# Layer-1 batch statistics of a four-layer graph network: one aggregation for each group of four batches in place of two for each batch

## The chip, the cores and the metric

The kernel runs on one core of a Trainium2 chip. Its time is the device time of one execution, in microseconds (us); the kernel before takes 2887.32 us, the median of three runs from 2887.09 to 2894.89. One further execution was profiled; its span is 2889.8 us. In the text the engines carry the names of the profile: PE (matrix multiply; PEld is its weight load), DVE (vector), ACT (scalar), POOL (GpSimd), SP (the queue that issues most transfers).

## What is computed

Four layers, each `x = x + layer(relu(layernorm(x)))`, on x of shape (128 batches, 128 nodes, 128 features), with a 0/1 adjacency of the same leading shape. The change lies in layer 1, whose reference, cut to what matters, is

```python
D = jnp.abs(x[:, :, None, :] - x[:, None, :, :])
h = jnp.einsum('bijc,oc->bijo', D, W1) + b1      # 64 outputs for each pair of nodes
m = jnp.mean(h, axis=(0, 1, 2))                  # over all batches and all pairs
v = jnp.mean((h - m) ** 2, axis=(0, 1, 2))
h = (h - m) / jnp.sqrt(v + EPS) * g1 + be1
...                                              # leaky relu, score, softmax, aggregation
```

The mean and the variance of h run over all 128 batches and all 128 x 128 pairs (i, j), so no h can be normalised before the last one exists. That is why the kernel has a first stage that only makes h and its statistics.

## The kernel before, in words

**Stages.** The first stage (about 80 to 1600 us of the span) computes h for every pair, keeps its statistics and writes h to DRAM (`HP`), and beside that runs layer 0 for the batches ahead. A short stretch of small operations (L804 to L841) folds the statistics into one scale and one bias. The second stage (about 1610 to 2400 us) reads h back and does the rest of layer 1; layers 2 and 3 follow.

**Tiles of the first stage.** D is symmetric, so for each batch only the distances k = 1 to 64 between i and j (mod 128) are made: the upper half of the partitions holds k = 1 to 32, the lower half 33 to 64. A batch has NT = 4 tiles of KC = 8 distances; i counts the tiles of all batches (512), b = i // 4 is the batch and t = i % 4 the tile in it. Four batches (G = 4) make a group of 16 tiles, the unit in which layer 0 runs. Since k = 64 meets each pair twice, it counts with half the weight of the others; it sits in the last 128 columns of the last tile of a batch.

For each tile, with the step names of the code:

- `d` (L585) takes the difference of x and its shifted copy. In tiles 1 and 3 of a batch POOL does it, in tiles 0 and 2 DVE; tile 0 uses a maximum in place of the difference. DVE reads x out of PSUM (`XP`, two tiles, one for each pair of batches, in turns), POOL out of SBUF.
- `abs` (L624, ACT) takes the absolute value in place; tile 0 of a batch has none.
- `hp` (L595 and, in tile 0 alone, also L598; PE) multiplies by W1 into one of two PSUM buffers (`big`, bufs=2), so hp of tile i can start when `hs` of tile i-2 has emptied its buffer.
- `hs` (L608, ACT) copies the result to SBUF.
- `st` (L615 to L620, DVE) takes its statistics: two bn_stats for each tile, of 512 columns each. In the last tile of a batch the second one covers only 384 columns, a third one takes the last 128 (k = 64), and two bn_aggr turn the nine triples of the batch into a mean and a variance of all and of the last k alone (`ST1[:, b, 0]`, `ST1[:, b, 1]`).
- `out` (SP) writes the batch's h to DRAM.

Other steps of the stage: for each pair of batches, number n, `xp<n>` (L652, PE, transposes x into XP), `xe<n>` (L656, ACT, copies it to SBUF), `again<n>` (L669, POOL, appends the first 64 columns again), `pw<n>` (L660, PE, a product with W1 into another part of the same XP tile), `xw<n>` (L664, ACT, reads that part). For each group, layer 0: `mask`, `rs`, `most`, `share`, `rso`, `m8`, `rsx` on POOL, `mv`, `deg`, `o`, `mvo`, `on`, `end`, `mvx`, `per` on DVE, `hn`, `hT`, `maskT`, `hw`, `oc`, `h1` on ACT, `pt`, `pm`, `ph`, `po` on PE.

**What sets the order.** Every step is entered in a list with an engine, an assumed cost in us, the steps it must follow, a rank (when it is due) and its work. `_ordered` (L113) runs a list schedule over that: it always takes the step that could start first by the assumed costs, the lower rank at a tie, and emits them in that order. Nothing is sorted again afterwards: each engine works off its queue in that order and waits at the head of it. The costs are entries in the planner only; they change no instruction, but they decide the order of every queue.

In the steady part the order repeats from group to group. With tiles 0 to 15 for a group, negative numbers for tiles of the group before, xw<1> for the second pair of batches of this group, <2> and <3> for those of the next, and (1), (2), (3) for layer 0 of one, two and three groups ahead, the order of the kernel before is

```
DVE  d0 st-4 d2 st-3 o(1) st-2 mvo(1) st-1 d4 st0 st1 mv(2) d6 st2 deg(2) on(1) st3 d8 end(1) st4 mvx(1)
     st5 d10 per(2) st6 st7 d12 st8 st9 d14 st10 st11
ACT  hs0 abs3 hs1 oc(1) hs2 xw<1> hs3 abs5 abs6 hs4 abs7 hs5 hs6 hn(2) hs7 abs9 hs8 hs9 abs10 abs11 h1(1)
     hT(2) hs10 h1(1) xe<2> abs13 hs11 hs12 abs14 maskT(2) xw<2> abs15 hw(2) hs13 hs14 xe<3> abs17 hs15 abs18
PE   hp0 hp1 hp2 pw<1> hp3 hp4 hp5 hp6 hp7 hp8 hp9 pt(2) hp10 hp11 xp<2> hp12 pm(2) ph(2) pw<2> hp13 hp14
     xp<3> po(2) hp15
POOL d1 again<1> d3 rso(1) d5 d7 rs(2) d9 most(2) d11 rsx(1) d13 share(2) d15 again<2> mask(3) m8(3)
```

In both kernels xw<2> (ACT) is emitted just after the d0 of the next group (DVE) and waits for it, and that d0 waits for pw<2> (PE): all three touch the same PSUM tile XP.

Of the kernel before, what the change touches and what calls it, by code (L numbers as in the profile page):

```python
# [9 lines left out]
F32 = mybir.dt.float32  # L10
# [7 lines left out]
P = 128  # L18
G = 4
# [8 lines left out]
KH = 32  # L28
# [6 lines left out]
NT = KH // KC  # L35
# [131 lines left out]
def tile_gnn_stack(ctx: ExitStack, tc: tile.TileContext, a: dict, out: bass.AP):  # L167
    nc = tc.nc
    NB = a["x"].shape[0]
    NG = NB // G  # L170

    const = ctx.enter_context(tc.tile_pool(name="const", bufs=1))
    res = ctx.enter_context(tc.tile_pool(name="res", bufs=1))
    small = ctx.enter_context(tc.tile_pool(name="small", bufs=4))
# [7 lines left out]
    def sm(name, tag="sm"):  # L182
        return psum.tile([P, G, P], F32, tag=tag, bufs=banks[tag], name=name)
# [28 lines left out]
    M8 = [res.tile([P, G, P], U8, tag=f"m{g}", name=f"m{g}") for g in range(NG)]  # L212
    MV1 = res.tile([P, NG, G, 2], F32, name="MV1")
    RS1 = res.tile([P, NG, G], F32, name="RS1")
    ST1 = res.tile([P, NB, 2, 2], F32, name="ST1")
    ST2 = res.tile([P, NG, 6], F32, name="ST2")

    def rsqrt(dst, var):

        nc.gpsimd.tensor_scalar(dst, var, EPS, None, op0=OP.add)  # L220
        nc.gpsimd.tensor_tensor(dst, dst, mhalf[:, 0:1].to_broadcast(list(dst.shape)), OP.pow)  # L221
# [35 lines left out]
    with tc.tile_pool(name="c0", bufs=1) as c0, tc.tile_pool(name="p0", bufs=2) as p0:  # L257
# [311 lines left out]
        def step(name, engine, cost, after, rank, work, takes=(), gives=()):  # L569
            steps.append((name, engine, cost, after, takes, gives, rank, work))  # L570

        XE, XW, diffs, linear, halves, stats = {}, {}, {}, {}, {}, {}

        def difference(i):

            b, t = divmod(i, NT)
            xe, k = XE[b // 2], b % 2
            on_pool = t in ON_POOL
            d = p0.tile([P, 2, KC, P], F32, tag=f"d{int(on_pool)}", name="d")
            x = xe[:, k, 0:P] if on_pool else XP[b // 2 % 2][:, k, :]  # L580
            ahead = xe[:, k, 1 + KC * t:]
            ahead = bass.AP(tensor=ahead.tensor, offset=ahead.offset,
                            ap=[list(ahead.ap[0]), [KH, 2], [1, KC], [1, P]])
            eng = nc.gpsimd if on_pool else nc.vector
            eng.tensor_tensor(d, ahead, x[:, None, None, :].to_broadcast([P, 2, KC, P]),  # L585
                              OP.max if t == BY_MAX else OP.subtract)
            diffs[i] = d.rearrange("p h k i -> p h (k i)")

        def products(i):
            d = diffs.pop(i)  # L590
            hp = linear[i] = big("hp").rearrange("p a b -> p (a b)")
            by_max = i % NT == BY_MAX
            for c in range(0, KC * P, 512):
                for hh in range(2):
                    nc.tensor.matmul(hp[64 * hh:64 * hh + 64, c:c + 512], w1T2 if by_max else w1T,  # L595
                                     d[:, hh, c:c + 512], start=True, stop=not by_max, skip_group_check=True)
                for hh in range(2 * by_max):
                    nc.tensor.matmul(hp[64 * hh:64 * hh + 64, c:c + 512], XW[i // NT // 2][:, i // NT % 2, :],  # L598
                                     both_t.rearrange("p h k i -> p h (k i)")[:, hh, c:c + 512],
                                     start=False, stop=True, skip_group_check=True)  # L600

        def evacuate(i):

            b, t = divmod(i, NT)
            if t == 0:
                halves[b] = p0.tile([P, NT, KC * P], F32, name="hs", bufs=3)
                stats[b] = small.tile([P, 9, 6], F32, name="st")
            nc.scalar.copy(halves[b][:, t, :], linear.pop(i))  # L608

        def statistics(i):  # L610

            b, t = divmod(i, NT)
            last = t == NT - 1
            hs, st = halves[b][:, t, :], stats[b]
            nc.vector.bn_stats(st[:, 2 * t, :], hs[:, 0:512])  # L615
            nc.vector.bn_stats(st[:, 2 * t + 1, :], hs[:, 512:1024 - P * last])  # L616
            if last:
                nc.vector.bn_stats(st[:, 8, :], hs[:, 1024 - P:])
                nc.vector.bn_aggr(ST1[:, b, 0, :], st.rearrange("p a b -> p (a b)"))
                nc.vector.bn_aggr(ST1[:, b, 1, :], st[:, 8, :])  # L620
                del stats[b]

        def absolute(i):
            nc.scalar.activation(diffs[i], diffs[i], AF.Abs)  # L624

        def pairs(i):

            b, t = divmod(i, NT)
            n, by_max = b // 2, t == BY_MAX
            engine, cost, rank = ("Pool", 4.25, i - 3) if t in ON_POOL else ("DVE", 2.2, i - 2)  # L630
            step(("d", i), engine, cost, [("again", n), ("d", i - 2), ("hp", i - 4)], rank, lambda: difference(i))
            if not by_max:
                step(("abs", i), "ACT", 1.8, [("d", i)], i - 1, lambda: absolute(i))
            step(("hp", i), "PE", 3.44 if by_max else 1.72,
                 [("d" if by_max else "abs", i), ("hp", i - 1), ("hs", i - 2)] + [("xw", n)] * by_max,
                 i, lambda: products(i))
            step(("hs", i), "ACT", 0.9, [("hp", i), ("hs", i - 1)]
                 + [("st", i - 2 * NT - 1), ("out", b - 3)] * (t == 0), i + 1, lambda: evacuate(i))
            step(("st", i), "DVE", 1.8 if t == NT - 1 else 1.2, [("hs", i), ("st", i - 1)], i + 2,
                 lambda: statistics(i))  # L640
            if t == NT - 1:
                step(("out", b), "SP", 0.4, [("hs", i)], i + 1.5, lambda: nc.sync.dma_start(HP[b], halves[b]))
# [154 lines left out]
        for i in range(NT * NB):  # L797
            pairs(i)
# [5 lines left out]
    with tc.tile_pool(name="bn", bufs=1) as bn:  # L804


        w_all, w_last, n = 2.0 * KH * P, -1.0 * P, 1.0 * NB * P * P
        last = bn.tile([P, 1], F32, name="last")
        nc.vector.memset(last[0:64, :], 0.0)
        nc.vector.memset(last[64:128, :], w_last)  # L810

        def fold_sum(t):

            acc = bn.tile([P, NB], F32, name="acc")
            nc.vector.tensor_scalar(acc, t[:, :, 0], w_all, None, op0=OP.mult)
            nc.vector.scalar_tensor_tensor(acc, t[:, :, 1], last[:, 0:1], acc, op0=OP.mult, op1=OP.add)
            tot = bn.tile([P, 1], F32, name="tot")
            nc.vector.tensor_reduce(tot, acc, AX.X, OP.add)
            pf = sm("pf")
            nc.tensor.matmul(pf[:, 0, 0:1], fold.rearrange("p a b -> p (a b)"), tot, start=True, stop=True)  # L820
            got = bn.tile([P, 1], F32, name="got", bufs=2)
            nc.vector.tensor_scalar(got, pf[:, 0, 0:1], 1.0 / n, None, op0=OP.mult)
            return got

        m = fold_sum(ST1[:, :, :, 0])
        dev = bn.tile([P, NB, 2], F32, name="dev")
        nc.vector.tensor_scalar(dev, ST1[:, :, :, 0], m[:, 0:1], None, op0=OP.subtract)
        nc.vector.tensor_tensor(dev, dev, dev, OP.mult)
        nc.vector.tensor_tensor(dev, dev, ST1[:, :, :, 1], OP.add)
        v = fold_sum(dev)  # L830
        mm = bn.tile([P, 1], F32, name="mm")
        nc.vector.tensor_tensor(mm, m, m, OP.mult)
        nc.vector.scalar_tensor_tensor(v, mm, NB * P / n, v, op0=OP.mult, op1=OP.add)
        scale1 = const.tile([P, 1], F32, name="scale1")
        bias1 = const.tile([P, 1], F32, name="bias1")
        rsqrt(scale1, v)
        nc.vector.tensor_tensor(scale1, scale1, g1, OP.mult)

        nc.vector.tensor_tensor(m, m, b1, OP.add)
        nc.vector.tensor_tensor(bias1, b1, m, OP.subtract)  # L840
        nc.vector.scalar_tensor_tensor(bias1, bias1, scale1[:, 0:1], be1, op0=OP.mult, op1=OP.add)  # L841
# [8 lines left out]
    with tc.tile_pool(name="c1", bufs=1) as c1, tc.tile_pool(name="p1", bufs=2) as p1:  # L850
# [34 lines left out]
        for n in range(2):  # L885
            t = c1.tile([P, G, 1 + 2 * KH], F32, name=f"sk{n}")
# [683 lines left out]
```

## Time and profile before

| what | value |
|---|---|
| median of three runs | 2887.32 us |
| span of the profiled execution | 2889.8 us |
| busy share of the span: PE, DVE, ACT, POOL | 85%, 87%, 83%, 60% |
| first stage: DVE, ACT, POOL, PE busy in 1000 to 1500 us | 473.62, 459.35, 453.83, 450.03 us |
| bn_stats L615 x512, L616 x512, L618 x128 | 681, 642 and 276 ns each |
| bn_aggr L619 x128 (54 numbers for each partition) | 399 ns each |
| bn_aggr L620 x128 (6 numbers) | 124 ns each |
| second stage, 1700 to 2300 us | DMA busy all the time, 409 GB/s |

A group of instructions is named by its line, its engine and the tiles it writes and reads; st<-hs is the statistics' bn_stats, ST<-st the bn_aggr. Idle time of an engine is put down to the instruction that ended the wait. The chain of waits goes back from the last instruction, at each step to what released it, and is then told in order of time.

### The profile page before, as it was taken

Reading aid. Unit: us, or ns where it says so; the run is one execution under the profiler, and the core shown is the slowest. Engines: PE = TensorE matmul, PEld = TensorE weight load, DVE = VectorE, ACT = ScalarE, POOL = GpSimd, SP = SyncE. Lnnn points to the kernel's source line nnn. Section 1 sums busy time; section 2 is a strip of 40 time slices with the busy share of each in tenths; the row PEclk is TensorE's granted clock in tenths of the full one; section 3 lists DMA queues with packets and bytes.
Section 4 is the critical chain, followed back from the end, with each engine's and each line's share of the span. In section 5 each row is a group of like instructions: output and inputs, shape, how many; then the busy total and the mean of one; then the engine's idle time right before and its main releaser. Section 6 shows DMA issues by size and latency. Waiting matters only on the chain.

```text
span 2889.8 us, 41921 instructions
## 1 busy us (share of the span) xinstructions
PE 2469.7 (85%) x14517; PEld 1185.7 (41%) x14517; DVE 2520.0 (87%) x4949; ACT 2392.2 (83%) x2811; POOL 1729.1 (60%) x1613
## 2 busy tenths in 40 slices
PE   1899899999898989898989688888888886998897
PEld 1333333333333333333333234444444444777675
DVE  5799999999999999999999578888888885987886
ACT  1799998989899999999999678777877774988886
POOL 2899989898989899898988001101111104665552
PEclk8899999999999999999999899999999997999998
DMA  5555545454544444454544999999999971111210
GB/s 200 201 202 221 204 190 204 190 204 190 204 193 200 195 199 200 193 207 186 215 171 204 368 408 408 410 409 409 410 410 410 408 283 54 45 59 63 63 34 27
DMA packets 180083, 653.83 MB, mean 226 GB/s; under 512 B 30992, under 2 KB 99472, under 8 KB 129680
## 3 DMA queue, kind: packets, MB, share of 16 engines
q1 hardware_dynamic: 179280, 646.80, 56.3%
q10 hardware_dynamic: 576, 4.19, 0.4%
q8 instruction: 119, 1.95, 0.3%
q14 instruction: 108, 0.88, 0.1%
HBM read 338.14 MB, written 312.80 MB: 225 GB/s over the span
## 4 chain that ended last, share of the span: by engine, by line
PE 36%; ACT 23%; DMA 20%; DVE 12%; issue 5%; POOL 3%; SPq 0%; DVEq 0%; ACTq 0%; POOLq 0%
PE hp L595 17%; ACT d L624 11%; DMA z<-hp 7%; DMA rows<-sk 7%; PE hp L598 5%; ACT hs L608 5%; DMA u<-rows 5%; DVE d L585 3%; PE pv L1292 2%; ACT o L717 2%; PE ps L919 1%; ACT h L1176 1%; DVE z L962 1%; PE po L741 1%; POOL rs L221 1%
## 5 line engine op out<-in xcount | busy, mean ns | idle before, releaser
L585 POOL TENSOR_TENSOR d<-xe 128x2048 f32<-128x2048 f32 x256 | 1074.0, 4201 | 86.2 <-PE hp L595 65.7
L595 PE MATMUL hp<-d,w1T 128*64 128x512 f32 x4096 | 1019.2, 621 | 123.1 <-ACT d L624 65.4
L624 ACT ACTIVATE d<-d 128x2048 f32<-128x2048 f32 x384 | 730.9, 1922 | 9.2 <-POOL d L585 5.0
L585 DVE TENSOR_TENSOR d<-xe,xp 128x2048 f32<-128x2048 f32 x256 | 579.9, 2265 | 28.6 <-PE xp L660 21.2
L608 ACT COPY hs<-hp 128x1024 f32<-128x1024 f32 x512 | 512.1, 1017 | 80.2 <-PE hp L598 43.3
L595 PEld LDWEIGHTS hp<-d,w1T 128*64 128x64 f32 x4096 | 290.9, 142 | 691.7 <-issue 465.3
L1008 POOL TENSOR_TENSOR x<-x,bt 128x512 f32<-128x512 f32 x32 | 43.7, 1366 | 684.7 <-DMA x<-x 684.7
L615 DVE BATCH_NORM_STATS2 st<-hs 128x6 f32<-128x512 f32 x512 | 348.8, 681 | 51.6 <-ACT hs L608 51.6
L616 DVE BATCH_NORM_STATS2 st<-hs 128x6 f32<-128x512 f32 (+1 forms) x512 | 328.7, 642 | 0.0
L962 DVE SCALAR_TENSOR_TENSOR z<-z 128x2048 f32<-128x2048 f32 x128 | 297.0, 2320 | 22.8 <-ACT z L944 22.8
L944 ACT ACTIVATE z<-z,bias,scale 128x2048 f32<-128x2048 f32 x128 | 267.3, 2088 | 18.8 <-DMA z<-hp 18.8
L948 ACT ACTIVATE zr<-z,bias,scale 128x2048 f32<-128x2048 f32 x128 | 267.4, 2089 | 9.7 <-DMA z<-hp 7.5
L598 PE MATMUL hp<-both_t,xw 128*64 128x512 f32 x1024 | 266.2, 594 | 0.0
L919 PE MATMUL ps<-z,w2z 128*32 128x512 f32 x1024 | 141.7, 626 | 83.2 <-DVE z L962 83.2
L926 PEld LDWEIGHTS pk<-pick,su 128*128 128x128 f32 x1024 | 125.7, 193 | 139.9 <-DVE su L940 103.0
L926 PE MATMUL pk<-pick,su 128*128 128x16 f32 x1024 | 138.2, 267 | 25.8 <-DVE su L940 24.7
L1292 PE MATMUL pv<-wr,e 128*128 128x128 f32 x1024 | 148.4, 293 | 10.7 <-DVE e L1269 6.1
L1292 PEld LDWEIGHTS pv<-wr,e 128*128 128x128 f32 x1024 | 133.8, 204 | 19.7 <-issue 3.8
L919 PE MATMUL ps<-z,w2l 128*32 128x512 f32 x1024 | 139.1, 612 | 0.6 <-DMA z<-hp 0.6
L919 PE MATMUL ps<-zr,w2r 128*32 128x512 f32 x1024 | 139.0, 615 | 0.4 <-ACT zr L948 0.4
L598 PEld LDWEIGHTS hp<-both_t,xw 128*64 128x64 f32 x1024 | 78.1, 138 | 143.1 <-issue 142.5
L1269 DVE SCALAR_TENSOR_TENSOR e<-e,ps 128x512 f32<-128x512 f32 x160 | 106.8, 678 | 28.7 <-ACT ps L1266 27.9
(266 smaller groups left out, 3855.5 us busy)
## 6 DMA issues: line engine op xcount, KB each, us to landing
hp<-hs SPq DMA_DIRECT2D x128, 2048.0 KB, 6.3
z<-hp SPq DMA_DIRECT2D x256, 1024.0 KB, 14.8
x<-x SPq DMA_DIRECT2D x128, 256.0 KB, 4.8
u<-rows SPq DMA_DIRECT2D x32, 384.0 KB, 11.6
x<-in_x_dram SPq DMA_DIRECT2D x32, 256.0 KB, 3.0
adj<-in_adj_dram SPq DMA_DIRECT2D x32, 256.0 KB, 3.4
out_dram<-x SPq DMA_DIRECT2D x32, 256.0 KB, 2.5
agg<-a SPq DMA_DIRECT2D x30, 256.0 KB, 3.8
```

The costliest lines, as they stand in the source:

```text
L585: eng.tensor_tensor(d, ahead, x[:, None, None, :].to_broadcast([P, 2, KC, P]), OP.max if t == BY_MAX else OP.subtract)
L595: nc.tensor.matmul(hp[64 * hh:64 * hh + 64, c:c + 512], w1T2 if by_max else w1T, d[:, hh, c:c + 512], start=True, stop=not by_max, skip_gr ...
L598: nc.tensor.matmul(hp[64 * hh:64 * hh + 64, c:c + 512], XW[i // NT // 2][:, i // NT % 2, :], both_t.rearrange("p h k i -> p h (k i)")[:, h ...
L608: nc.scalar.copy(halves[b][:, t, :], linear.pop(i))
L615: nc.vector.bn_stats(st[:, 2 * t, :], hs[:, 0:512])
L616: nc.vector.bn_stats(st[:, 2 * t + 1, :], hs[:, 512:1024 - P * last])
L624: nc.scalar.activation(diffs[i], diffs[i], AF.Abs)
L919: nc.tensor.matmul(ps[32 * c:32 * c + 32, :], w[:, w0:w0 + 32], v[:, 512 * c:512 * c + 512], start=j0 == 0, stop=w is w2r, skip_group_chec ...
L944: nc.scalar.activation(z0, z0, AF.Identity, bias=bias1, scale=scale1[:, 0:1])
L948: nc.scalar.activation(zr, z1, AF.Relu, bias=bias1, scale=scale1[:, 0:1])
L962: nc.vector.scalar_tensor_tensor(z0, z0, 0.01, z0, op0=OP.mult, op1=OP.max)
L1292: nc.tensor.matmul(t[pv][:, k % 2, hd, :], t[e][:, hd, :], flat[:, at:at + P], start=True, stop=True)
```

## The change

The statistics tile `st` now belongs to a group of four batches. Its triples lie so that all of one batch's position come side by side over the four batches, and the ninth position (k = 64) has its four batches together. The bn_stats are the same as before. The two bn_aggr run only after the last tile of the last batch of a group: one over the 8 x 4 triples of k = 1 to 63 (192 numbers for each partition), one over the 4 triples of the last k (24 numbers). `ST1` has 32 entries in place of 128, the weights and tiles of the fold after the stage follow suit, and three costs in the planner's list are new. It is meant to spare the DVE small instructions.

```diff
-    ST1 = res.tile([P, NB, 2, 2], F32, name="ST1")
+    ST1 = res.tile([P, NG, 2, 2], F32, name="ST1")
...
-                stats[b] = small.tile([P, 9, 6], F32, name="st")
+                if b % G == 0:
+                    stats[b // G] = p0.tile([P, 2 * NT + 1, G, 6], F32, name="st")
...
-            hs, st = halves[b][:, t, :], stats[b]
+            hs, st = halves[b][:, t, :], stats[b // G][:, :, b % G, :]
             nc.vector.bn_stats(st[:, 2 * t, :], hs[:, 0:512])
             nc.vector.bn_stats(st[:, 2 * t + 1, :], hs[:, 512:1024 - P * last])
             if last:
-                nc.vector.bn_stats(st[:, 8, :], hs[:, 1024 - P:])
-                nc.vector.bn_aggr(ST1[:, b, 0, :], st.rearrange("p a b -> p (a b)"))
-                nc.vector.bn_aggr(ST1[:, b, 1, :], st[:, 8, :])
-                del stats[b]
+                nc.vector.bn_stats(st[:, 2 * NT, :], hs[:, 1024 - P:])
+            if last and b % G == G - 1:
+                of_all = stats.pop(b // G).rearrange("p a g b -> p a (g b)")
+                nc.vector.bn_aggr(ST1[:, b // G, 0, :], of_all[:, 0:2 * NT, :].rearrange("p a b -> p (a b)"))
+                nc.vector.bn_aggr(ST1[:, b // G, 1, :], of_all[:, 2 * NT, :])
...
-            step(("st", i), "DVE", 1.8 if t == NT - 1 else 1.2, [("hs", i), ("st", i - 1)], i + 2,
+            step(("st", i), "DVE", (1.5 if b % G < G - 1 else 2.8) if t == NT - 1 else 1.35, [("hs", i), ("st", i - 1)], i + 2,
                  lambda: statistics(i))
...
-        w_all, w_last, n = 2.0 * KH * P, -1.0 * P, 1.0 * NB * P * P
+        w_all, w_last, n = 2.0 * G * (KH - 1) * P, 1.0 * G * P, 1.0 * NB * P * P
         last = bn.tile([P, 1], F32, name="last")
-        nc.vector.memset(last[0:64, :], 0.0)
+        nc.vector.memset(last[0:64, :], 2 * w_last)
         nc.vector.memset(last[64:128, :], w_last)
...
-            acc = bn.tile([P, NB], F32, name="acc")
+            acc = bn.tile([P, NG], F32, name="acc")
...
-        dev = bn.tile([P, NB, 2], F32, name="dev")
+        dev = bn.tile([P, NG, 2], F32, name="dev")
```

With the new costs the planner emits another order, again the same in every group of the steady part:

```
DVE  d0 st-4 st-3 o(1) d2 st-2 mvo(1) st-1 d4 st0 st1 mv(2) d6 st2 deg(2) on(1) st3 d8 end(1) st4 mvx(1)
     st5 d10 per(2) st6 st7 d12 st8 st9 d14 st10 st11
ACT  hs0 abs3 hs1 oc(1) hs2 xe<1> hs3 abs5 hs4 xw<1> abs7 abs6 hs5 hn(2) hs6 abs9 hs7 hT(2) hs8 abs11 abs10
     hs9 h1(1) h1(1) abs13 hs10 xe<2> hs11 maskT(2) hw(2) abs14 hs12 xw<2> abs15 hs13 hs14 abs17 hs15 abs18
PE   hp0 hp1 xp<1> hp2 hp3 hp4 pw<1> hp5 hp6 hp7 pt(2) hp8 hp9 ph(2) hp10 hp11 xp<2> pm(2) hp12 pw<2> hp13
     po(2) hp14 hp15
POOL d1 d3 rso(1) d5 d7 again<1> rs(2) d9 most(2) d11 rsx(1) d13 share(2) d15 again<2> mask(3) m8(3)
```

## The prediction

> **What bounds the kernel now.** I read the busy times by stretch first. The two rows below are each one group of the first stage, from d0 to d0 on DVE; columns: stretch, length, then busy time of PE, PEld, DVE, ACT, POOL, the granted PE clock, the DMA share and GB/s.
>
> ```profile
> 263.92:310.31 46.39, 41.74 (x206) 16.11 (x206) 45.06 (x82) 43.65 (x48) 43.23 (x27) 1.00 0.50 204
> 789.42:837.22 47.80, 43.14 (x206) 16.58 (x206) 45.17 (x83) 43.88 (x48) 43.27 (x27) 0.96 0.49 198
> ```
>
> DVE is the fullest engine (45.1 us of each group), but no engine is full, and the two groups do the same work in times that differ by 1.41 us: the later one has a PE clock of 0.96. So a group is paced by a loop of waits through the queues. The chain of waits shows it (start, us, what; the first line is from an early group):
>
> ```profile
> 300.64 3.74 PE hp L595 x16
> ...
> 885.01 2.30 DVE d L585
> 887.30 0.02 issue
> 887.33 0.28 ACT xw L664
> 887.60 1.80 ACT d L624
> 889.40 0.50 ACT hw L730
> ...
> 919.76 1.92 ACT d L624
> 921.69 0.04 issue
> 921.73 5.13 PE hp L595 x16
> ...
> 932.79 2.30 DVE d L585
> ```
>
> The loop passes DVE only in d0; the statistics aren't on it. And after the wait for abs10, hp10 and hp11 (x16) take 5.13 us where they took 3.74. Last, who waits for whom (360 to 1500 us: sum, times, longest):
>
> ```profile
> PE hp L595 <- ACT d L624: 55.8, 24, 2.3
> ...
> DVE st L615 <- ACT hs L608: 40.5, 47, 1.0
> ...
> ACT xw L664 <- DVE d L585: 22.7, 24, 0.9
> ...
> DVE d L585 <- PE xp L660: 14.2, 24, 0.6
> ```
>
> Each wait comes once or twice in each of 24 groups. PE stands 2.3 us before hp10; DVE itself idles 2.3 us a group, for hs and for pw<2>.
>
> [...] xw<2> on ACT waits for the d0 that reads the same XP tile, 0.9 us in each group. [...] from about 700 us on the groups take 47.79. The loop needs 46.39 us; the slow stretch adds 5.13 - 3.74 = 1.39; the sum is 14 windows. The group has locked to them: a later start within the window shortens the slow part, an earlier one lengthens it.
>
> **The change part by part.** On DVE, the end of a batch and its queue, by the timeline:
>
> ```profile
> 895.44 0.55 DVE L616 BATCH_NORM_STATS2 st<-hs 128x6 f32<-128x384 f32 x1
> 895.90 0.28 DVE L618 BATCH_NORM_STATS2 st<-hs 128x6 f32<-128x128 f32 x1
> 896.21 0.40 DVE L619 BATCH_NORM_AGGREGATE ST<-st 128x2 f32<-128x54 f32 x1
> 896.53 0.12 DVE L620 BATCH_NORM_AGGREGATE ST<-st 128x2 f32<-128x6 f32 x1
> 896.57 2.25 DVE L585 TENSOR_TENSOR d<-xe,xp 128x2048 f32<-128x2048 f32 x1
> ```
>
> From L618 to d takes 0.67 us. In three batches of four it will be L618 alone: four such bn_stats (L694) take 0.86 us together, so 0.19 each; 3 x 0.48 = 1.4 us saved. In the fourth the aggregation grows. From 6 to 54 numbers its time goes from 124 to 399 ns, 5.7 ns a number; 192 then cost 1.19 us and 24 cost 0.23. Less the overlap of 0.08 seen above and with one more wait between them that is 1.7 us in place of 0.67: 1.0 added. Net 0.4 us a group (bounds: 1.4 saved if the cost were per instruction, 0.2 added if 192 numbers cost half as much again). None of it is on the loop: the long aggregation stands before d4, and hp4, which needs d4, waits 0.9 us longer for hs2 (below). The fold (L815 to L829) shrinks from 128 to 32 columns, about 1 us less in once-only operations of 0.2 to 0.4 us, and the last aggregation, which nothing hides, adds 1.0: zero.
>
> What counts is the order. Four moves matter: st-3 and o now stand before d2, not behind it; abs7 stands before abs6; both h1 and abs13 stand between hs9 and hs10; ph moves away from pm. I walk the loop of the new order with durations of the trace. First the old order as a test, from d0: xw 2.32; abs-1, hw 2.62; po 1.75; hp-1, hp0 5.20; 0.22 to hs0; ACT to abs5 7.12; abs5, abs6 3.61; hs4, abs7 2.71; hs5 to hp7 1.17; hp7, hp8 5.17; hp9 to hs9 1.96; hs9 0.90; abs10 to hp10 1.97; hp10, hp11 3.67; xp 0.37; hp12 3.58; pm, ph 1.39; pw to d0 0.66. Sum 46.39: the early groups exactly. The new one, each edge a queue order or a true dependence:
>
> ```
> from d0                                                      us      sum
> xw<0> after d0 2.32; abs-1 1.97                             4.29     4.29
> hs-3 to st-3 1.04; st-3 1.20; o 0.59                        2.83     7.12   st-3 before d2
> d2 to abs2 2.32; abs2 1.82                                  4.14    11.26
> hs0, abs3, hs1, oc                                          5.16    16.42
> hs2 to hp4 1.06; hp4 3.48; to hs4 0.22                      4.76    21.18   PSUM buffer of hp2
> hs4 0.90; xw<1> 0.17; abs7 1.81; abs6 to hp6 1.97           4.85    26.03   abs7 before abs6
> hp6, hp7 3.67; pt 0.55; hp8 3.48                            7.70    33.73
> to hs8 0.24; hs8 0.91; abs11, abs10 3.61; hs9 0.91          5.67    39.40
> h1 1.54; abs13 1.81                                         3.35    42.75   before hs10
> hs10 to hp12 1.08; hp12 3.52; pw<2> to d0 0.66              5.26    48.01   PSUM buffer of hp10
> ```
>
> (d4 is ready at 16.6, before hp4's 17.5.) So the new loop needs at least 48.0 us, 1.6 more than the old one with the clock undisturbed, and 0.2 more than what the old one takes now.
>
> The clock: PE now stands about 2.5 us before hp6 (hp5 ends near 23.4) and 2.1 us before hp10; the old order had one such gap, 2.33. With 48.0 above 14 windows the new group can't lock: it drifts 0.22 us later in the window each time until a gap lies badly, loses about 1.6 us once (as 5.35 against 3.74 in the group at 347 us), and is past it. Walking one window of 3.41 us takes some seven groups of 0.22 and one of 1.8, so 0.43 above 14 windows on average; with the second gap I take 48.3.
>
> Sum: from d0 at 263.92 to d0 at 1506.23 are 26 groups in 1242.3 us; at 48.3 they take 1255.8, +13.5. About two groups before that ran unslowed and get 1.9 each, +4. Together +17.5: 2905. The walk's own bounds: 48.0 throughout, 26 x 0.22 + 2 x 1.6 = +9, 2896; 48.8, 26 x 1.0 + 2 x 2.4 = +31, 2918. The second stage is bound by its transfers (409 GB/s) and only starts later.
>
> **The rivals.** (1) DVE is the bound, being busiest: 32 x 0.4 = 13 us saved, 2874. For it: 94% busy, and 40.5 us of waits for hs that a freer queue may use. Against it: these waits are DVE's own idleness, and the old loop has no statistics in it. An order that also loses the slow clock would give 26 x 1.4 = 36 us, 2851; but hs8, abs11, abs10 before hp10 keep a gap of over 2 us. Slower is my forecast, so this rival ends on the other side. (2) My walk is some 0.3 us too long; then the group locks to 14 windows again as now, and only the early groups lose, 2 x 1.4: 2890, no change that can be told. For it: the lock is strong, and 48.0 is only 0.2 above it. Against: the same durations gave the old loop to 0.01. (3) The gap before hp6 slows the clock in nearly every group, 48.0 + 1.6 = 49.6: 26 x 1.8 + 2 x 3.2 = +53, 2940. For it: that gap is longer than the old one and hp6 to hp8 lie on the loop. Against: in the early groups of before a gap of 2.33 did no harm.
>
> **How the numbers follow.** The loop with an occasional slow clock 0.60, rival 1 0.12, rival 2 0.15, rival 3 0.13. A change within 0.3% is 2879 to 2896; the low end of the first case touches it, 0.05, so slower 0.55 + 0.13 = 0.68; rival 2 and that end 0.20; rival 1 0.12. The range from 2882 to 2934 leaves out most of rival 1 and the upper half of rival 3, 2 in 10. The unknown cost of bn_aggr moves none of it, since d4 has 0.9 us to spare.
>
> **What would show it.** The distance of d0 to d0 on DVE: 48.0 us in undisturbed groups, some with 1.6 more, mean 48.3. The chain with st-3, o, d2 in each group, and abs7, abs6 before hp6. PE idle 2.5 us before hp6 for ACT abs. bn_aggr at 1.19 and 0.23 us, 32 each, DVE's busy time down by about 13 us while its idle time grows. I am wrong if groups take 47.8 or less, or if the chain runs through DVE's statistics.

## The result and the profile after

The changed kernel takes 2927.21 us, the median of 5 runs (2924.65 to 2935.45), against 2889.08 us before (5 runs, 2887.09 to 2894.89): a ratio of 1.0136, 95% interval 1.0119 to 1.0154. It is slower by 38 us where 17.5 were forecast. The profiled spans are 2926.1 and 2889.8 us.

First the stretches of the changed kernel: one group that the slow clock hit, the next that it did not hit, and 26 groups in a row, each from d0 to d0 (columns as in the prediction: stretch, length, busy time of PE, PEld, DVE, ACT, POOL, granted PE clock, DMA share, GB/s).

```profile
858.87:909.59 50.72, 45.39 (x206) 16.90 (x204) 44.54 (x76) 43.67 (x48) 42.13 (x26) 0.93 0.45 183
909.59:957.68 48.09, 42.24 (x206) 16.16 (x206) 44.31 (x76) 43.61 (x48) 43.95 (x27) 1.00 0.48 194
...
270.99:1547.86 1276.87, 1131.70 (x5306) 428.08 (x5306) 1154.28 (x1977) 1139.12 (x1223) 1122.43 (x676) 0.97 0.47 192
```

An undisturbed group takes 48.08 us (forecast 48.01), with a full clock; a disturbed one takes 50.72. Of these 26 groups 10 are disturbed, at every second or third place, 15 take 48.08, and one 48.44 (it waits for `mask` on POOL). The mean is 1276.87 / 26 = 49.11 us, against 48.3 forecast and 1242.3 / 26 = 47.78 before.

The chain of waits of the changed kernel (start, us, what), with an undisturbed group up to 858.87 (the one of 48.44 us; up to hp10 it runs like the others) and a disturbed one after it:

```profile
810.43 2.30 DVE d L585
...
816.38 0.68 DVE st L617
817.06 0.59 DVE o L746
817.65 2.19 DVE d L585
...
836.49 3.65 PE hp L595 x16
...
849.04 3.68 PE hp L595 x16
...
858.87 2.30 DVE d L585
...
884.93 5.35 PE hp L595 x16
...
899.17 5.38 PE hp L595 x16
...
904.68 4.20 POOL d L585
908.88 0.24 POOL xe L671
...
909.59 2.30 DVE d L585
```

st-3 and o stand before d2, as the walk had it, and hp6 starts 836.49 - 810.43 = 26.06 us after d0 (walk: 26.03). In the disturbed group both stretches are slow, hp6 and hp7 (x16) by 5.35 - 3.65 = 1.70 us and hp10 and hp11 (x16) by 5.38 - 3.68 = 1.70 us. From the second the chain goes over POOL: d15 (904.68), again<2> (908.88), then d16 on DVE. That edge isn't in the walk.

The same disturbed group, cut where its granted PE clock changes (columns as above; the clock is the third number from the end):

```profile
858.87:885.89 27.02, 23.60 (x116) 8.97 (x114) 25.07 (x45) 23.60 (x25) 24.39 (x15) 1.00 0.44 185
885.89:889.30 3.41, 3.41 (x12) 0.97 (x10) 3.41 (x7) 2.98 (x6) 1.77 (x2) 0.50 0.20 75
889.30:899.54 10.24, 8.32 (x44) 3.32 (x42) 9.94 (x19) 7.71 (x7) 8.77 (x6) 1.00 0.49 205
899.54:902.95 3.41, 3.41 (x10) 0.97 (x8) 1.67 (x3) 3.41 (x6) 2.29 (x2) 0.50 0.03 8
902.95:909.59 6.64, 6.64 (x36) 2.67 (x34) 4.45 (x6) 5.97 (x8) 4.91 (x3) 1.00 0.79 288
```

Each loss of 1.70 us is one stretch of 3.41 us in which PE is busy throughout at half its clock. The two stretches begin 13.65 us apart, four times 3.41. From 110 us of the span on, the granted clock of this trace and of that of the kernel before changes only at moments of one grid, 3.41 us apart; one step of it is a window, here and in the prediction. In the kernel before, 25 slow stretches in a row begin 47.79 us apart, 14 x 3.413; the first of them and two later ones (columns as above):

```profile
347.89:351.30 3.41, 3.41 (x10) 0.96 (x8) 3.41 (x5) 3.41 (x7) 3.41 (x2) 0.50 0.00 0
825.76:829.17 3.41, 3.02 (x8) 1.00 (x10) 3.41 (x5) 3.39 (x5) 3.41 (x1) 0.50 0.00 0
829.17:873.54 44.37, 40.12 (x198) 15.57 (x194) 41.74 (x79) 40.47 (x43) 39.83 (x27) 1.00 0.52 213
873.54:876.95 3.41, 3.01 (x8) 1.00 (x10) 3.41 (x5) 3.39 (x5) 3.41 (x1) 0.50 0.00 0
```

The lock is there to be seen: hp10 starts at 347.04, 0.85 us ahead of the first, takes 5.35 us (x16, with hp11), and the next hp10 comes 48.01 us later; at 826.15 it starts 0.39 us behind the slow stretch's start, takes 5.13, and the next comes after 47.79.

Who waits for whom in the changed kernel, 360 to 1500 us (sum, times, longest):

```profile
POOL d L585 <- PE hp L595: 102.0, 79, 2.9
...
PE hp L595 <- ACT d L626: 100.0, 46, 2.4
...
DVE st L616 <- ACT hs L609: 54.8, 43, 1.9
...
ACT xw L666 <- DVE d L585: 43.6, 23, 2.2
```

PE's waits for abs have gone from 24 to 46, two in each group, and DVE and ACT stand idle for longer. The work that was saved is there all the same; on DVE, at the end of a group (start, us, engine, line, operation):

```profile
823.04 0.28 DVE L619 BATCH_NORM_STATS2 st<-hs 128x6 f32<-128x128 f32 x1
823.24 1.00 DVE L622 BATCH_NORM_AGGREGATE ST<-st 128x2 f32<-128x192 f32 x1
824.16 0.20 DVE L623 BATCH_NORM_AGGREGATE ST<-st 128x2 f32<-128x24 f32 x1
824.28 2.23 DVE L585 TENSOR_TENSOR d<-xe,xp 128x2048 f32<-128x2048 f32 x1
```

The two kinds of bn_aggr take 32 x (1.004 + 0.205) = 38.7 us in all, where 128 x (0.399 + 0.124) = 66.9 us were spent before. DVE's busy time falls from 2520.0 to 2493.7 us and the kernel is slower.

Where the time went, in order: the first of the 26 groups starts 7.1 us later than the one it answers to before (270.99 against 263.92; the groups ahead of it are longer), the 26 groups add 34.6, the rest of the stage 4.8. The second stage, from the start of its first ACT operation on z (the tile into which h is read back) to that of its last, starts 46.4 us later (1655.6 against 1609.2), but takes 747.6 us where it took 755.4, so 7.8 come back. What follows is 2.2 us shorter in these two executions, which leaves the 36.3 us between the spans.

### The profile page after: what moved, and what is told of

The parts are those of the page before. It is cut to its first block, busy times and chain, and to the rows that moved or that the text cites. A ratio compares the mean times of both kernels' runs of the same rounds, so it can differ in the third digit from the quotient of the medians.

```text
span 2926.1 us, 41825 instructions
## 1 busy us (share of the span) xinstructions
PE 2487.6 (85%) x14517; PEld 1184.7 (40%) x14517; DVE 2493.7 (85%) x4757; ACT 2391.1 (82%) x2811; POOL 1718.9 (59%) x1613
## 4 chain that ended last, share of the span: by engine, by line
DVE 33%; PE 29%; ACT 15%; DMA 9%; POOL 9%; issue 4%; SPq 0%; DVEq 0%; POOLq 0%; ACTq 0%
PE hp L595 12%; DVE d L585 9%; ACT d L626 8%; POOL d L585 5%; PE ps L921 5%; DVE st L617 3%; DVE z L964 3%; DMA rows<-sk 3%; DMA z<-hp 3%; DVE st L616 3%; DMA u<-rows 2%; PE hp L598 2%; PE pv L1294 2%; ACT hs L609 2%; PE pk L928 2%
```

## The experiments

The theory at this point: the order alone makes the loss, by a loop of 48.08 us and a slow clock behind two waits of PE; the aggregation is worth nothing in the first stage. Rivals: the longer aggregation holds DVE's queue up; or the slow stretches only lie beside a path that DVE sets.

**The two halves of the change.** The kernel before with the planner's three new costs and nothing else (its instructions are those of before in the new order), and the changed kernel with the old costs (the new aggregation in the old order).

```diff
-            step(("st", i), "DVE", 1.8 if t == NT - 1 else 1.2, ...
+            step(("st", i), "DVE", (1.5 if b % G < G - 1 else 2.8) if t == NT - 1 else 1.35, ...
```

> The kernel before with only the planner's three costs changed: the aggregations stay two for each batch, the order of every queue becomes that of the changed kernel. Theory (the order and the clock make the loss): as the changed kernel, 2927 us give or take 6, groups of 48.1 and 50.7 us. Rival A (the one long aggregation, 1.2 us in front of d4, makes the loss): as before, 2889. Rival B (both, half each): about 2908.

> The changed kernel with the old costs: one aggregation for four batches, the order of before. Theory: groups lock to 47.79 us again and the spared 0.4 us a group become idle time of DVE: 2888 us give or take 3. Rival A (long aggregation makes the loss): about 2927. Rival C (DVE is the bound of the stage): 13 us less, 2876.

The order alone: 2931.81 us, ratio 1.0152 (1.0135 to 1.0169), groups of 48.09 and 50.73 us. It has the old bn_aggr after every batch, more DVE work than the changed kernel, and the same group to 0.01 us. The aggregation alone: 2882.44 us, ratio 0.9981 (0.9971 to 0.9991); its groups take 48.0, then 47.79, no shorter than before, and its gain lies in the second stage (748.0 us); in all it is 3 us below the range that was expected. So the order makes the whole loss.

The first run also settles a doubt, since the prediction names a chain through DVE's statistics as a sign of being wrong. Between d2 and hp6 the chain of the changed kernel runs down DVE's queue, through st and ST, to the `o` that ends at 834.49, and then to an abs at 834.53. By the code that abs needs only d6, which ended at 832.10; and ACT was busy in its own queue up to it with another abs:

```profile
832.56 0.28 ACT L666 ACTIVATE xw<-xp 128x128 f32<-128x128 f32 x1
832.73 3.71 ACT L626 ACTIVATE d<-d 128x2048 f32<-128x2048 f32 x2
```

abs7 and abs6 lie back to back here. DVE's queue and ACT's come to the same moment within 0.04 us, and the chain names DVE. In the run of the order alone DVE comes to this `o` half a microsecond earlier (22.83 us after d0, against 23.37), since the short bn_aggr stands before d4 in place of the long one. There the chain names ACT, hs4, xw<1>, abs7, abs6, and hp6 starts just as late, 836.99 - 810.93 = 26.06 us after d0:

```profile
810.93 2.30 DVE d L585
...
832.15 1.01 ACT hs L608
833.16 0.18 ACT xw L664
833.34 1.29 ACT d L624
...
835.03 1.92 ACT d L624
...
836.99 5.35 PE hp L595 x16
```

So ACT sets the start of hp6. The long aggregation uses up the room that DVE had there, and no more.

**Filling PE's waits.** By the theory, the clock stays up if PE does something in its wait. Products that nobody reads are put ahead of hp10, or hp6 and hp10, into the buffer that the next product overwrites. They are work added; nothing is left out.

```diff
+            for _ in range(4 * (i % (G * NT) in (10,))):     # (6, 10) in the changed kernel; later 2 in place of 4
+                nc.tensor.matmul(hp[0:64, 0:512], w1T, both_t.rearrange("p h k i -> p (h k i)")[:, 0:512],
+                                 start=True, stop=True, skip_group_check=True)
```

> The kernel before with four matmuls more in front of hp10 of each group, into the buffer that hp10 then overwrites, 1.7 us of PE work in the 2.3 us in which PE waits for abs10: work added, none left out. Theory (the wait slows the clock, the clock costs 1.39 us a group): groups of 46.4 us all through, 26 x 1.39 = 36 less, 2853 us, PE clock 1.00 in the stage. Rival D (the slow stretch is hidden or has another cause than the idle PE): 2889 or more.

> The changed kernel with four matmuls more in front of hp6 and of hp10 of each group, in the two waits of PE for abs. Theory: every group takes the 48.08 us of the undisturbed ones, 12 x 2.64 = 32 less than the changed kernel, 2895 us, still slower than before by the order alone. Rival D (the clock isn't the cause): 2927 or more. If the order alone made no loss without the clock: 2853 as the third run.

Both missed: 2884.45 us (0.9996, 0.9987 to 1.0005) and 2951.44 us (1.0226, 1.0209 to 1.0243). A filler shows in the trace as two matmul records (passes, in the expectations) of 0.43 us each, not of the 0.22 that one takes in hp, where 16 take 3.65. Four fillers are 3.45 us in a wait of 2.33, so hp10 comes late: the groups of the first kernel take 47.34 = 46.39 + 0.95 throughout, those of the second 49.54. No group of either is disturbed, but the price hides what was to be seen. Two fillers (1.73 us) fit:

> As the third run with two extra matmuls in place of four. There each took 0.86 us (two passes of 0.43), 3.45 us in a wait of 2.33, so hp10 began late by 0.95 us and the groups took 46.39 + 0.95 = 47.34. Two take 1.73 us and fit. Theory: no slow stretch and no delay, groups of 46.4 us, 26 x 1.39 = 36 less than before, 2850 us. Rival (a remaining wait of 0.6 us, or PE's work as such, still brings the slow clock): 47.8 again, 2886.

> The changed kernel with two extra matmuls in front of hp6 and of hp10. Theory: all groups at 48.1 us, 12 x 2.64 = 32 less than the changed kernel: 2895 us, 9 over before: that would be the order's own loss without the clock. Rival (the order's loss is all clock): 46.4 us groups, 2850.

The kernel before with them takes 2849.81 us (0.9876, 0.9858 to 0.9895), with groups of 46.39 throughout, the sum of the old walk. The changed kernel takes 2897.63 us (1.0041, 1.0026 to 1.0057), with groups of 48.08 (one of 48.44, for `mask` again). Their stretches from 360 to 1500 us, first the kernel before with fillers:

```profile
360.00:1500.00 1140.00, 1071.07 (x5111) 407.42 (x5113) 1107.34 (x2017) 1072.67 (x1154) 1056.57 (x633) 1.00 0.50 203
```

and the changed kernel with fillers:

```profile
360.00:1500.00 1140.00, 1085.38 (x5026) 407.04 (x5024) 1049.00 (x1800) 1034.48 (x1113) 1025.07 (x616) 1.00 0.49 197
```

The granted clock is 1.00 in both. This splits the result: with the clock left full the changed kernel is 2897.6 - 2849.8 = 47.8 us slower. The slow clock costs the kernel before 2885.0 - 2849.8 = 35 us. It costs the changed one some 26 to 30: 26.4 us in the 26 groups (1276.87 against 1250.52), 2927.2 - 2897.6 = 29.6 in all, of runs on two occasions, between which the kernel before differs by 4 us. So the clock costs the changed kernel no more than the kernel before; it loses because its loop is 1.7 us longer *and* it still pays for the clock.

**The best of both.** The aggregation in the old order, with two fillers ahead of hp10:

> The old order, one aggregation for four batches and two extra matmuls in front of hp10. Theory: groups of 46.4 us as in the fifth run (the spared 0.4 us of DVE a group is not on the loop), and the 4 us that the second run was below before: 2846 us. Rival (without the slow clock DVE becomes the bound, and sparing it pays 13 us): 2837.

2846.05 us, ratio 0.9868 (0.9848 to 0.9888), groups of 46.38: faster than both kernels. DVE is not the bound even here, since its shorter work again changes no group.

**One move of the order taken back.** In the changed kernel's plan, abs7 is put behind abs6 again.

```diff
-            for work in _ordered(steps, {"sm": 2}):
+            plan = _ordered(steps, {"sm": 2})
...
+            for i in range(6, NT * NB, G * NT):
+                first, second = names.index(("abs", i + 1)), names.index(("abs", i))
+                if first < second:
+                    plan.insert(second, plan.pop(first))
...
+            for _, work in plan:
```

> The changed kernel with one move undone: abs6 stands before abs7 on ACT again. Theory, from the sum of the loop: hp6 starts 1.8 us earlier, its wait shrinks to 0.7 us, hp7 then waits for hs5, hp8 starts 0.9 us earlier; groups of 47.2 us undisturbed, one long wait left (before hp10), so they lock to 47.8 or stay near 47.2: 2872 to 2892 us. Rival (st-3 and o before d2, or h1 before abs13, is the costly move): 2915 or more.

2888.77 us, 1.0014 (1.0004 to 1.0024). The wait before hp6 is cut to under a microsecond and the one before hp10 stays, as PE's queue shows (last column: idle before, and what ended it):

```profile
913.74 1.94 PE L595 MATMUL hp<-d,w1T 128*64 128x512 f32 x8 [0.64 <-ACT d L626]
916.53 1.94 PE L595 MATMUL hp<-d,w1T 128*64 128x512 f32 x8 [0.86 <-ACT hs L609]
...
927.36 3.65 PE L595 MATMUL hp<-d,w1T 128*64 128x512 f32 x16 [1.92 <-ACT d L626]
```

The groups take 47.36 and about 48.2 us, mostly in turns; the mean is 47.79, the 14 windows again. So with a wait left, the loops of 46.39 and 47.36 us, shorter than 14 windows, were held at 14 on average (47.79 us), and the one of 48.08 us drifts. Undisturbed groups are 48.08 - 47.36 = 0.72 us shorter by this one move; the other 0.97 us over the old 46.39 come with the rest of the new order, whose moves were not taken back one by one.

**What each slow stretch costs.** The changed kernel with two fillers ahead of hp6 alone, and ahead of hp10 alone.

> The changed kernel with two unused products of 64x512 ahead of hp6 alone, so that only the wait ahead of hp10 can slow the clock. Theory (slow hp10 and hp11 are on the path through hp11, d15 and d16): undisturbed groups 48.1, disturbed ones longer by 1.0 to 1.7, with hp6 and hp7 x16 at 3.65 in all; since a smaller loss is left over, the bad place of the window comes back at other intervals; mean 48.3 to 48.9, so 2903 to 2919 us. Rival (the losses lie in slow hp6 and hp7): groups 48.1 throughout, 2898.

> The changed kernel with two unused products of 64x512 ahead of hp10 alone, so that only the wait ahead of hp6 can slow the clock. Theory (each of the two waits costs by itself): disturbed groups longer by 0.9 to 1.7, hp10 and hp11 x16 at 3.65 in all, mean 48.3 to 48.9, 2903 to 2919 us. Rival (the losses lie in slow hp10 and hp11 alone): groups 48.1 throughout, 2898.

2909.28 us (1.0070, 1.0053 to 1.0087) and 2908.29 us (1.0067, 1.0050 to 1.0085): each wait costs by itself, and both rivals (2898) are out. A disturbed group with fillers ahead of hp6, hp6 and then hp10:

```profile
878.29 3.65 PE L598 MATMUL hp<-d,w1T 128*64 128x512 f32 x16 [0.72 <-ACT d L629]
...
890.84 5.35 PE L598 MATMUL hp<-d,w1T 128*64 128x512 f32 x16 [1.92 <-ACT d L629]
```

and one with fillers ahead of hp10:

```profile
876.68 5.35 PE L598 MATMUL hp<-d,w1T 128*64 128x512 f32 x16 [2.43 <-ACT d L629]
...
890.92 3.65 PE L598 MATMUL hp<-d,w1T 128*64 128x512 f32 x16
```

In the first, disturbed groups take 49.02 us, 0.95 more than 48.07; in the second 49.77, 1.70 more. The slow hp6 and hp7 cost all of their 1.70 us, the slow hp10 and hp11 0.95 of theirs, and 1.70 + 0.95 = 2.65 is what a disturbed group of the changed kernel loses, 2.64. With fillers ahead of hp10 they come at every fifth or sixth place, five of 26; with fillers ahead of hp6 six of 26 are disturbed, four of them in two pairs.

**The second stage.** The smaller `ST1` (1536 bytes less for each partition) and the `st` tiles that leave the pool `small` (896 bytes with their rounding) put all tiles of the second stage 2432 bytes lower. Where the new aggregation is in, that stage took 747.5 to 749.3 us, in eight kernels; with the old one 753.5 to 755.4, in four. An unused tile in front moves the tiles back:

```diff
     keep = ctx.enter_context(tc.tile_pool(name="keep", bufs=1))
+    room = keep.tile([P, 600], F32, name="room")        # then 608
+    nc.vector.memset(room, 0.0)
```

> The statistics in groups in the order before (as in the run of that part alone), with one unused tile of 2400 bytes a partition put ahead of the second stage's tiles, as many bytes as the change frees there (1536 by the smaller ST1, 864 by the four small st tiles), so that the tiles of the second stage lie again where they lie in the kernel before; the room is filled once with zeros on DVE and never read. Theory that the second stage is shorter because its tiles lie 2400 bytes lower: first to last z 754 to 756 us again, 2887 to 2891 us in all. Rival, that it is shorter because of something else (the shorter sums of the statistics, the state in which the first stage ends): 747 to 749 us as before, 2880 to 2885 in all.

> As the run before with the room, but of 2432 bytes, with which the tiles of the second stage begin at exactly the offset of the kernel before (71648 bytes in a partition for the first z; 69216 in the changed kernel, 71616 with a room of 2400, which gave 750.3 us from the first to the last z and 2887.0 in all). Theory that the offset of the tiles sets the 7.8 us: 754 to 756 us from first to last z, 2887 to 2891 in all. Rival (the offset does nothing; the second stage varies by some us with the moment at which its transfers begin): 747 to 751 us, and 2880 to 2887 in all.

The first, 32 bytes off the old offset, fell between the two: 750.3 us in the stage, 2886.96 in all (0.9990, 0.9981 to 0.9999). At the old offset it is 754.0 us and 2886.47 in all (1.0000, 0.9990 to 1.0010; the total is half a microsecond under what was expected). From the first to the last z, the kernel with the new aggregation in the old order:

```profile
1610.70:2358.70 748.00, 656.52 (x4880) 308.17 (x4884) 617.92 (x939) 590.79 (x397) 70.02 (x60) 0.95 1.02 410
```

and the same with the room of 2432 bytes:

```profile
1607.70:2361.70 754.00, 648.02 (x4878) 303.79 (x4878) 621.66 (x939) 591.51 (x398) 81.97 (x60) 0.96 1.02 407
```

The same transfers move at 410 and at 407 GB/s. So the offset of the tiles accounts for 6 us of the 7.8; each stage length is that of one profiled execution. What in the offset does it (a boundary, a neighbour) wasn't tried and stays open.

## Why the prediction was wrong, point by point

**What held.** The direction, and that only the order counts: the order alone gives 1.0152. The walk: 48.01 forecast, 48.08 measured, hp6 at 26.06 us for 26.03; and the old one, 46.39, which the kernel before shows throughout once the clock is left full. The aggregation is worth zero in the first stage; its costs were too high (1.19 and 0.23 us forecast, 1.00 and 0.20 measured, so 26 us less DVE work where 13 were forecast), which moved nothing. The gaps of PE: 2.5 and 2.1 us forecast, 2.43 and 1.92 measured. The lock of the old loop to 14 windows (14 x 3.413 = 47.79 us between its slow stretches): fill the wait and the kernel is 1.2% faster.

**The step that failed** is the one on the clock: "it drifts 0.22 us later in the window each time until a gap lies badly, loses about 1.6 us once ..., and is past it", with "with the second gap I take 48.3". The drift and the loss are there, but the loss was mis-sized. A loop that is longer than 14 windows by a drift, and that loses a fixed time where it lies badly, comes round, by the author's estimate, after N groups with N x drift + loss = one window. The traces give 3.41 us for that: the slow stretches are 3.41 us long and lie on a grid of 3.41 us, two groups of 48.08 + 50.72 are 98.80 us = 28.95 windows, three of 48.08 + 48.08 + 50.72 are 43.03. The mean is then 14 windows + 3.41 / N:

```
                          drift   loss   N = (3.41 - loss) / drift   mean = 47.79 + 3.41 / N   measured
forecast                   0.22    1.6    8.2                         48.2 (48.3 taken)
fillers ahead of hp10      0.29    1.70   5.9                         48.4                      48.41, 5 of 26
fillers ahead of hp6       0.29    0.95   8.5                         48.2                      48.30, 6 of 26
changed kernel             0.29    2.64   2.7                         49.1                      49.11, 10 of 26
```

The formula takes one loss to carry the wait past the bad places. With fillers ahead of hp6 it doesn't hold: a loss of 0.95 us leaves the wait among them in two of four passes through the window, so that the next group is hit too, and 6 groups are disturbed where the formula has 3.

With the loss of 2.64 in place of 1.6 and the drift as forecast, N is 3.5 and the mean 48.8: a little over half of the miss. The drift of 0.29 brings the rest, together with that loss; with a loss of 1.6 it gives 48.3. Two things made the loss 2.64. Both waits fall badly in the same group, where the prediction gave the second gap 0.1 us a group without a sum: the groups take 48.41 us on average with that wait filled and 49.11 with it open, 0.70 more. The chain shows hp10 14.24 us behind hp6 in a disturbed group, 12.55 in an undisturbed one, so the first loss carries the second wait on by half a window. The traces show that this takes it into the bad part; what makes that part bad, they don't show. Take the start of a slow stretch as the start of a window, and count in windows of 3.41 us. With fillers ahead of hp6, a wait before hp10 that begins at 0.08 to 0.46 of a window is followed by the slow clock, and one that begins at 0.57 to 1.06 is not. In the changed kernel's disturbed groups it begins at 0.22 to 0.33; half a window earlier that would be 0.72 to 0.83, where it did no harm. And the walk passes hp10 and hp11 by, since hs10 waits for abs13 anyway; it lacked the edge from hp11 over POOL's d15 and again<2> to d16, by which 0.95 us arrives. With one wait left (fillers ahead of hp10) the kernel takes 2908.29 us, close to the 2905 forecast for two.

For the sum: 26 groups gave +34.6 where +13.5 was forecast, the groups before them +7.1 for +4.

**A second step failed the other way**: "The second stage ... only starts later". It is 7.8 us shorter, most of it by the lower offset of its tiles. The change to `ST1` and `st` was costed as instructions alone and not as a change of where everything behind them lies. Without this the result would have been further off.

**The rivals.** DVE as the bound (2874) fell with the first two runs. The lock (2890) needs a loop under 47.79; it came as soon as abs7 was moved back (2888.77). Nearly every group slow (49.6, 2940) was nearer than the forecast in size, for a reason that it did not have: not every group, but 10 of 26 with both waits slow.

## What to carry to other kernels

When an edit also changes a planner's costs, price the two apart: here the instructions saved were worth nothing (1.0000 with the tiles at their old offset), and three numbers that only steer the order cost 1.5%. In a periodic kernel, compare the period with multiples of the grid on which PE's clock changes (3.41 us in these traces), follow what a slow stretch behind each of PE's waits (1.92 to 2.43 us here) delays, by all routes to the period's end, and use N = (3.41 - loss) / drift to estimate how often it is paid (it came out in two kernels of three here); two products that nobody reads, where they fit into the wait, won 1.2%. A tile that shrinks moves the tiles behind it (by 2432 bytes here, worth 6 us of the second stage), so the stages that the edit does not touch must be measured too.

## What the runs showed of the hardware that was not expected

- Behind a wait of PE of 1.92 us the products were slow, x16 in 5.35 us for 3.65, but only in some places of the window (waits that begin at 0.08 to 0.46 of it, with fillers ahead of hp6): in the changed kernel the same wait is harmless in 16 of 26 groups. With the waits cut by 1.73 us of products the granted clock was 1.00 from 360 to 1500 us.
- The slow clock came in stretches of 3.41 us at 0.50, and one that lay wholly on running products cost them 1.70 us. In the old order it began before hp10 (825.76 against 826.15) and cost 5.13 - 3.74 = 1.39.
- A 64x512 float32 product shows as two matmul records; alone they took 0.43 us each, in hp, where the two column halves take turns, 0.22 to 0.23 each (3.65 / 16).
- bn_aggr over 192 numbers for each partition took 1.00 us, over 54 0.40 us, over 24 0.20 us, over 6 0.12 us: from 54 to 192, (1004 - 399) / 138 = 4.4 ns a number.
- The second stage, in which the DMA engines are busy throughout (share 1.02, 407 to 410 GB/s), took 748.0 us with its tiles at one offset and 754.0 us with the same tiles 2432 bytes higher.
